# Fourier blocks of 80 instead of 48 in a two-layer graph kernel, with the stages set in another order

## The chip, the cores and the metric

The kernel runs on one core of a Trainium2 chip. The metric is device time in microseconds (us) of one execution. The core has five engines with a queue of instructions each: TensorE (PE, matrix products; its weight loads are PEld), VectorE (DVE), ScalarE (ACT), GpSimd (POOL) and SyncE (SP, which here only issues DMAs). Each works its queue off in order and waits on semaphores where an operand comes from another engine or from a DMA. Matmuls write to PSUM, which has eight banks of 128 partitions by 512 float32; DVE and ACT empty them into SBUF.

## The reference, cut to what matters

The input is `x` of 128 graphs with 128 nodes and 256 channels, float32. Two layers are computed, each as x + layer(relu(layernorm(x))).

```
# layer 0, on h = relu(layernorm(x)) and its channels-first form hc
c = relu(bn1(conv1d(hc, conv1_w)))            # kernel size 1
x_conv = relu(bn2(conv1d(c, conv2_w, pad 8)) + hc)    # 17 taps along the nodes, 256 to 256 channels
s = h @ w_se.T + b_se;  A = exp(-|s_i - s_j|^2) * adj
x_nmp = A @ relu(h @ w_msg.T + b_msg)         # the neighbour part
gi = [x_conv, x_nmp] @ w_ih.T + b_ih;  gh = h @ w_hh.T + b_hh
r, z = sigmoid(gi_r + gh_r), sigmoid(gi_z + gh_z)
x = x + (1 - z) * tanh(gi_n + r * gh_n) + z * h
# layer 1, on the first 25 nodes of each graph: five groups of nodes, each two normalized graph
# convolutions (256 to 512 to 256) with relu, fused with softmax weights and added to x
```

The convolution with 17 taps is the largest piece. Both kernels compute it by a short Fourier transform along the nodes. The 128 nodes of a graph are cut into blocks of F - 16 outputs, each block is transformed with F points (a matmul with a constant matrix), each frequency is multiplied by the spectrum of the taps (a 256 by 256 complex product), and the result is transformed back.

## The kernel before, in words

With F = 48 a block gives OB = 32 outputs, so a graph has NB = 4 blocks, and 128 columns of a product hold BG = 32 graphs: NBAT = 4 batches of BQ = 8 groups. A group `q` is GB = 4 graphs; there are NQ = 32. There are NF + 1 = 24 frequency steps: the first holds the two real ones, and each of the other 23 a complex one as three real products.

The pieces of work are Python generators:

- `stage_a(q)` (L366) loads a group, normalizes it (`moments` L270, `normalize` L281), transposes it on PE (`ph`, L383), writes hT to DRAM (`hTd`, L390), does the first convolution (`pc`, L396; its eviction `h`, L399 and L401) and the forward transform (`pf`, L409; evicted by DVE at L415 and ACT at L417 into `X`).
- `tap_weights()` (L438) makes the tap spectra: 128 matmuls `pw` (L454) with 17 rows each on four groups of 32 rows, evicted by ACT (L457) and DVE (L458) into `ws`, which goes to DRAM as `wfd` (L463).
- `stage_b(bat)` (L476) does the products of one batch: it loads `wf` from `wfd`, forms sums on POOL (L496, L497), multiplies (`pa`, `pb`, L502), and writes `y` to DRAM as `yd`.
- `neighbours(q)` (L566) computes x_nmp (`pse` L572, `pm` L592, `pd` L604 and L606, `px` L617). `early(q)` (L623) does it ahead for the first batch and leaves the result in DRAM (`xmd`).
- `stage_n(q)` (L638) gets hT and x_nmp for the gates: from DRAM for the first batch, by computing the neighbour part for the others. `stage_c(q)` (L659) transforms back (`pi`, L678), computes the gates (products `p`, L713, and `pg`, L777), with Sigmoid and Tanh on ACT and the last sums on POOL, and writes out.
- `prepare(blk)` and `block(blk)` are layer 1, in eight blocks of 16 graphs (`py`, `ph`, `pz`, `pg`, `pfu`, from L1001 on). A block needs the four groups of gates that it covers.

The order in which all these stand in the engines' queues is fixed when the program is made. `Order.run` takes several lanes of generators. A generator yields two numbers: PE time that it has just put into the queue, and time until its next part can run. The lane that has received least PE time for its weight is next, if its next part is ready on this planned clock. `ahead` is the number of generators of a lane under way at once. Nothing is reordered on the chip.

Before, the first eight `stage_a` run beside `tap_weights`, then the products of batch 0 beside the eight `early`. After that the gates start, and transforms and products of batches 1 to 3 are a lane beside the gates (weight 0.5); layer 1 is a lane beside the gates once the last batch has its products:

```
    groups = Lane([stage(q) for q in range(NQ) for stage in (stage_n, stage_c)], ahead=2)
    side = Lane(first, weight=0.5)
    order.run(groups, side, beside, until=side)
    order.run(groups, Lane(second, ahead=2, weight=0.4))
```

Of the kernel before, what the change touches and what calls it, by code (L numbers as in the profile page):

```python
# [23 lines left out]
F = 48  # L24
# [6 lines left out]
HB = NB // 2 * F  # L31
# [28 lines left out]
def _fourier():  # L60
# [7 lines left out]
    inv = np.zeros((P, OB * NB // 2))  # L68
# [10 lines left out]
    for b in range(NB // 2):  # L79
        s = slice(b * OB, (b + 1) * OB)  # L80
        inv[b * F, s], inv[b * F + 1, s] = 1 / F, (-1.0) ** i / F
        for f in range(1, NF + 1):
            th = 2 * np.pi * ((f * i) % F) / F
            inv[b * F + 2 * f, s] = 2 / F * np.cos(th)
            inv[b * F + 2 * f + 1, s] = -2 / F * np.sin(th)
# [5 lines left out]
    tap4 = np.zeros((P, 64))  # L91
    for r in range(4):
        tap4[32 * r:32 * r + TAPS, :F] = tap
# [86 lines left out]
class Order:  # L180
# [6 lines left out]
    def run(self, *lanes, until=None):  # L187
        for lane in lanes:
            lane.done = 0.0
        while True:  # L190
# [13 lines left out]
            lane.done += step[0]  # L204
            r[1] = self.now + step[1]
# [3 lines left out]
def kernel(ctx: ExitStack, tc: tile.TileContext, x, adj, consts, vecs, w_se, conv1_w,  # L209
# [15 lines left out]
    xmd = [dr.tile([P, 2, 512], FP, name=f"xmd{q}") for q in range(BQ)]  # L225
# [25 lines left out]
    c1w = wp.tile([P, 2, D], FP, name="c1w")  # L251
# [12 lines left out]
    brow = cp.tile([P, D], FP, name="brow")  # L264
# [4 lines left out]
    def moments(src, tag):  # L269

        st = f2.tile([P, 4, 6], FP, tag=tag + "st", name="st")
        mv = f2.tile([P, 4, 2], FP, tag=tag + "mv", name="mv")
        rs = f2.tile([P, 4], FP, tag=tag + "rs", name="rs")
        for t in range(4):
            nc.vector.bn_stats(st[:, t], src[:, t])
            nc.vector.bn_aggr(mv[:, t], st[:, t])
        nc.vector.tensor_scalar(rs, mv[:, :, 1], EPS, None, op0=ALU.add)  # L277
        nc.gpsimd.tensor_tensor(rs, rs, c("mhalf")[:, :4], ALU.pow)  # L278
        return mv, rs
# [68 lines left out]
    lab = ExitStack()  # L348
    ab = lab.enter_context(tc.tile_pool(name="ab", bufs=2, side="right"))
    xf = lab.enter_context(tc.tile_pool(name="xf", bufs=1, side="right"))  # L350
    LATE = {}
    X = xf.tile([P, 2, F, P], FP, name="X")
    XA, MOM, LOADED = {}, {}, set()
    A_DONE, B_DONE, G_DONE, C_DONE = set(), set(), {-1}, set()

# [5 lines left out]
    def load_xa(q):  # L361
        LOADED.add(q)
        XA[q] = ab.tile([P, 4, D], FP, tag="xa", name=f"xa{q}")
        load_x(XA[q], q)

    def stage_a(q):  # L366

        while q // BQ and q // BQ - 1 not in B_DONE:
            yield 0.0, 1.0
        for n in range(q, min(q + 2, NQ)):  # L370
            if n not in LOADED:
                load_xa(n)
        if q not in MOM:
            MOM[q] = moments(XA[q], "a")
            normalize(XA[q], XA[q], *MOM[q])
            yield 0.0, 6.0
        xn = XA.pop(q)
        nxt = q + 1 if q + 1 < NQ else None
        hT = ab.tile([P, 2, 512], FP, tag="hTa", name=f"hTa{q}", bufs=1)
# [8 lines left out]
        if q + 2 < NQ:  # L388
            load_xa(q + 2)
        nc.gpsimd.dma_start(out=hTd[q], in_=hT)  # L390
        h1 = ab.tile([P, GB, D], FP, tag="h1", name=f"h1{q}", bufs=1)
        for h in range(2):
# [9 lines left out]
            if h and nxt:  # L402
                MOM[nxt] = moments(XA[nxt], "a")
            yield 1.75, 1.6 * h
        for h in range(2):
# [12 lines left out]
            if h and nxt:  # L418
                normalize(XA[nxt], XA[nxt], *MOM[nxt])
            yield 1.3, 1.5 * h  # L420
# [3 lines left out]
    mid = ExitStack()  # L424
# [4 lines left out]
    def load_taps(n, *engines):  # L429

        wt = tw.tile([P, 16, D], FP, tag="wt", name=f"wt{n}", bufs=4)
# [6 lines left out]
    def tap_weights():  # L438


        yield 0.0, 0.0
        for n in range(4):
            if n == 1:
                load_taps(3, nc.sync, nc.gpsimd)
                load_late()
            for m in range(8):
                if m % 4 == 0:
                    ws = tw.tile([P, 2, 8, D], FP, tag="ws", name=f"ws{n}_{m}")
                pws = [ptmp.tile([P, 2, D], FP, tag="tmp", name=f"pw{n}_{m}_{h}")
                       for h in range(2)]  # L450
                for r in range(4):
                    rows = slice(32 * r, 32 * r + TAPS)
                    o = r % 2 * 64
                    nc.tensor.matmul(pws[r // 2][o:o + 64], c("tap")[rows],  # L454
                                     wts[n][rows, 2 * m:2 * m + 2], start=True, stop=True)
                i = m % 4 * 2
                nc.scalar.activation(ws[:, 0, i:i + 2], pws[0], AF.Copy)  # L457
                nc.vector.tensor_copy(ws[:, 1, i:i + 2], pws[1])  # L458
                yield 0.9, 1.2
                if m % 4 == 3:  # L460
                    for r in range(4):
                        o, i0 = r % 2 * 64, 64 * r + 16 * n + 2 * (m - 3)
                        nc.gpsimd.dma_start(out=wfd[:, i0:i0 + 8], in_=ws[o:o + F, r // 2])  # L463
# [6 lines left out]
        LATE["io"] = ctx.enter_context(tc.tile_pool(name="io", bufs=2, reuse_waits="tile"))  # L470
        LATE["fr"] = ctx.enter_context(tc.tile_pool(name="fr", bufs=1, reuse_waits="tile"))
        LATE["xf"] = lab.enter_context(
            tc.tile_pool(name="xw", bufs=3, side="right", reuse_waits="tile"))


    def stage_b(bat):  # L476
        while not all(q in A_DONE for q in range(bat * BQ, (bat + 1) * BQ)):
            yield 0.0, 0.5
        while "xf" not in LATE:
            yield 0.0, 0.5  # L480
        if bat == 0:
            yield 0.0, 12.0
        WF, xf = {}, LATE["xf"]

        def load_w(f):
            w = WF[f] = xf.tile([P, 2, 3, D], FP, tag="wf", name=f"wf{bat}_{f}")
# [17 lines left out]
        for f in range(2):  # L504
            load_w(f)
        yield 0.0, 4.0
        late = None
        for f in range(NF + 1):
            if f + 2 <= NF:
                load_w(f + 2)  # L510
# [3 lines left out]
            pa = ptmp.tile([P, 2, D], FP, tag="tmp", name=f"pa{bat}_{f}")  # L514
# [21 lines left out]
    IN, IN2, X1, E_DONE = {}, {}, {}, set()  # L536
# [10 lines left out]
    def sums(name, q, x, bufs=1):  # L547


        t = LATE["fr"].tile([P, 4, D], FP, tag=name, name=f"{name}{q}", bufs=bufs)  # L550
# [6 lines left out]
    def load_yt(q, h):  # L557

        if q < NQ and q // BQ in B_DONE:
            IN2[q, h] = LATE["io"].tile([HB, GB, D], FP, tag="yt", name=f"yt{q}_{h}")  # L560
            x0 = (q % BQ * 2 + h) * GB
            nc.sync.dma_start(
                out=IN2[q, h],
                in_=yd[q // BQ].rearrange("(x b) f c -> (b f) x c", b=NB // 2)[:, x0:x0 + GB])
# [58 lines left out]
    def early(q):  # L623
# [3 lines left out]
        if q not in IN:  # L627
            IN[q] = load_n(q)
            yield 0.0, 6.0
        hT, ad = IN.pop(q)  # L630
        if q + 1 < BQ and q + 1 in A_DONE:
            IN[q + 1] = load_n(q + 1)
# [5 lines left out]
    def stage_n(q):  # L638
        if q < BQ:
            while len(E_DONE) < BQ:  # L640
                yield 0.0, 0.5
            hT = LATE["io"].tile([P, 2, 512], FP, tag="hT", name=f"hT{q}")
            nc.sync.dma_start(out=hT, in_=hTd[q])
            xm = LATE["fr"].tile([P, 2, 512], FP, tag="xnmp", name=f"xms{q}", bufs=2)
            nc.sync.dma_start(out=xm, in_=xmd[q])
            yield 0.0, 4.0
            HT[q] = hT
        else:
            while q not in A_DONE:
                yield 0.0, 1.0  # L650
            hT, ad = load_n(q)
            yield 0.0, 4.0
            HT[q] = hT
# [495 lines left out]
```

## Time and profile before

| | us |
|---|---|
| median of three runs | 2195.71 (2195.38 to 2197.89) |
| span of the profiled execution | 2200.9 |
| PE busy | 2117.9 |
| DVE, POOL, ACT busy | 1166.1, 791.8, 730.5 |
| products (L502 `pa`, `pb`), busy | 181.9, 94.5 |
| forward transforms (L409), busy | 99.7 |
| tap spectra on PE (L454), busy | 40.7 |
| DMA | 259.65 MB, mean 118 GB/s |

A row of the page gives line, engine, operation, names of the result and the operands, shapes, count, busy time and mean duration of one. A float32 matmul leaves two records on PE. Matmuls overlap in the pipeline, so the mean duration of a record is longer than the time that it holds PE; the latter is the distance from start to start in the timeline.

### The profile page before, as it was taken

The page shows a single profiled execution, that of the slowest core. Times are in us where ns is not written, and L with a number is a line of the kernel's source. Part 1 is how long each engine was busy: PE and PEld are TensorE (multiplying, and loading weights), DVE is VectorE, ACT ScalarE, POOL GpSimd, SP SyncE. Part 2 cuts the span into 40 slices and gives each one's busy share as a digit, 9 for nine tenths or more (in the row PEclk, how much of TensorE's full clock was granted, in tenths as well). Part 3 has the DMA queues.
Part 4 walks back from the last instruction along what each step waited for, and adds up shares of the span by engine and source line. Part 5 has one row for each costly group of instructions (what it writes and reads, how often), then busy time and mean ns, then how long its engine had stood idle before and what let it go on. Part 6 is the DMA issues. An engine that isn't in the chain of part 4 may idle for free.

```text
span 2200.9 us, 30725 instructions
## 1 busy us (share of the span) xinstructions
PE 2117.9 (96%) x11308; PEld 1678.9 (76%) x11308; DVE 1166.1 (53%) x2659; ACT 730.5 (33%) x1519; POOL 791.8 (36%) x978
## 2 busy tenths in 40 slices
PE   6979999999999999999999999899999999999997
PEld 3558868888888888888788888677786777877765
DVE  4544446645556555445665455655464555554442
ACT  2432233322234432334342323323334233233332
POOL 2217613355522245542224555413223323213330
PEclk9989999999999999999999999999999999999999
DMA  9868643455532344533224446222222223212221
GB/s 173 239 197 288 236 105 91 149 164 162 162 101 87 106 139 144 153 120 106 76 79 149 128 154 167 60 80 60 77 77 78 67 68 87 70 52 63 87 68 49
DMA packets 193977, 259.65 MB, mean 118 GB/s; under 512 B 21981, under 2 KB 157154, under 8 KB 192290
## 3 DMA queue, kind: packets, MB, share of 16 engines
q1 hardware_dynamic: 165682, 175.89, 28.2%
q0 software_dynamic: 27312, 81.03, 12.2%
q8 instruction: 90, 1.47, 0.3%
q10 hardware_dynamic: 832, 0.75, 0.2%
q14 instruction: 61, 0.50, 0.1%
HBM read 178.44 MB, written 79.17 MB: 117 GB/s over the span
## 4 chain that ended last, share of the span: by engine, by line
PE 86%; DVE 6%; DMA 3%; ACT 1%; POOL 1%; issue 1%; SPq 0%; DVEq 0%; ACTq 0%; POOLq 0%
PE p L713 34%; PE pa L502 8%; PE pg L777 5%; PE pm L592 4%; PE ph L1018 4%; PE pc L396 4%; PE pz L1027 4%; PE pb L502 4%; PE pf L409 3%; PE pi L678 2%; PE px L617 2%; PE pg L1060 1%; PE pc L692 1%; PE po L829 1%; PE py L1001 1%; PE ph L383 1%
## 5 line engine op out<-in xcount | busy, mean ns | idle before, releaser
L502 PE MATMUL pa<-wf,X 128*128 128x256 f32 x768 | 181.9, 380 | 0.0
L278 POOL TENSOR_TENSOR rs<-rs,cst 128x4 f32<-128x4 f32 x40 | 41.3, 1032 | 334.3 <-DVE rs L277 327.2
L502 PEld LDWEIGHTS pa<-wf,X 128*128 128x128 f32 x768 | 144.6, 190 | 22.1 <-issue 2.4
L813 POOL TENSOR_TENSOR d<-hT,r 128x512 f32<-128x512 f32 x64 | 82.2, 1285 | 215.0 <-ACT r L810 215.0
L525 DVE SCALAR_TENSOR_TENSOR y<-pa,kk 128x512 f32<-128x512 f32 x92 | 63.5, 690 | 156.0 <-ACT kk L524 155.9
L713 PE MATMUL p<-tc,wrz 128*128 128x256 f32 x512 | 132.0, 380 | 5.0 <-DVE tc L552 5.0
L713 PE MATMUL p<-th,wrz 128*128 128x256 f32 x512 | 134.1, 385 | 0.0
L713 PE MATMUL p<-tm,wrz 128*128 128x256 f32 x512 | 132.3, 381 | 0.0
L592 PE MATMUL pm<-wmsg,hT 128*128 128x256 f32 x512 | 123.7, 386 | 0.0
L497 POOL TENSOR_TENSOR wf<-wf 128x512 f32<-128x512 f32 x92 | 116.6, 1268 | 18.9 <-DMA wf<-wfd 18.9
L496 POOL TENSOR_TENSOR xs<-X 128x256 f32<-128x256 f32 x92 | 67.8, 737 | 154.6 <-PE pb L502 130.9
L396 PE MATMUL pc<-c1w,hTa 128*128 128x256 f32 x512 | 122.1, 385 | 0.2 <-DVE h L399 0.2
L777 PE MATMUL pg<-hT,whn 128*128 128x512 f32 x256 | 121.2, 599 | 0.0
L396 PEld LDWEIGHTS pc<-c1w,hTa 128*128 128x128 f32 x512 | 96.9, 192 | 22.6 <-ACT ws L457 5.7
L1018 PE MATMUL ph<-yz,w 128*128 128x96 f32 (+3 forms) x640 | 110.7, 326 | 3.4 <-DVE aT L609 1.6
L592 PEld LDWEIGHTS pm<-wmsg,hT 128*128 128x128 f32 x512 | 97.7, 194 | 20.9 <-issue 8.2
L713 PEld LDWEIGHTS p<-tc,wrz 128*128 128x128 f32 x512 | 97.5, 191 | 19.0 <-DVE tc L552 5.8
L524 ACT ACTIVATE kk<-pb 128x256 f32<-128x256 f32 x92 | 35.3, 383 | 225.5 <-PE pb L502 225.5
L1018 PEld LDWEIGHTS ph<-yz,w 128*128 128x128 f32 x640 | 88.1, 193 | 26.5 <-issue 15.7
L713 PEld LDWEIGHTS p<-tm,wrz 128*128 128x128 f32 x512 | 98.0, 191 | 13.4
L1027 PE MATMUL pz<-hh,w 128*128 128x96 f32 (+3 forms) x640 | 107.4, 322 | 0.0
L713 PEld LDWEIGHTS p<-th,wrz 128*128 128x128 f32 x512 | 94.8, 191 | 15.9 <-issue 3.5
(205 smaller groups left out, 4614.2 us busy)
## 6 DMA issues: line engine op xcount, KB each, us to landing
wf<-wfd SPq DMA_DIRECT2D x192, 256.0 KB, 3.2
yd<-y POOLq DMA_DIRECT2D x96, 256.0 KB, 2.5
yt<-yd SPq DMA_DIRECT2D x64, 384.0 KB, 4.4
hT<-hTd SPq DMA_DIRECT2D x40, 512.0 KB, 5.6
w<-in_W SPq DMA_DIRECT2D x40, 512.0 KB, 3.7
xa<-in_x SPq DMA_DIRECT2D x128, 128.0 KB, 4.6
hTd<-hTa POOLq DMA_DIRECT2D x32, 512.0 KB, 4.5
xt<-in_x SPq DMA_DIRECT2D x128, 128.0 KB, 2.8
```

The source lines that it names most:

```text
L396: nc.tensor.matmul(pc[:, i], hT[:, k, (2 * h + i) * N:(2 * h + i + 1) * N], c1w[:, k], start=(k == 0), stop=(k == 1))
L409: nc.tensor.matmul(pf[:, i, :F * NB], h1[:, 2 * h + i, k * P:(k + 1) * P], fwd, start=True, stop=True)
L496: nc.gpsimd.tensor_tensor(XS[f], X[:, :, 2 * f], X[:, :, 2 * f + 1], ALU.add)
L497: nc.gpsimd.tensor_tensor(WF[f][:, :, 2], WF[f][:, :, 0], WF[f][:, :, 1], ALU.add)
L502: nc.tensor.matmul(ps, xk(k), WF[f][:, k, s], start=(k == 0), stop=(k == 1))
L525: nc.vector.scalar_tensor_tensor(y, pa, 2.0, kk[:, None].to_broadcast([P, 2, D]), op0=ALU.mult, op1=ALU.subtract)
L592: nc.tensor.matmul(pm[:, i], hT[:, k, j * N:(j + 1) * N], wmsg[:, k], start=(k == 0), stop=(k == 1))
L713: nc.tensor.matmul(ps[:, m], w[:, i, k, m * P:(m + 1) * P], factor(i, x, t), start=first and j == 0, stop=last and j == len(n) - 1)
L777: nc.tensor.matmul(pg, whn[:, k, dc * P:(dc + 1) * P], hT[:, k], start=(k == 0), stop=(k == 1))
L813: nc.gpsimd.tensor_sub(d, hT[:, dc], r[:, dc])
L1018: nc.tensor.matmul(ph, w1[:, k, m * P:(m + 1) * P], yz[:, k, :, o:o + n], start=(k == 0), stop=(k == 1))
L1027: nc.tensor.matmul(pz, w2[:, g, m, cc * P:(cc + 1) * P], hs[g][:, m], start=(m == 0), stop=(m == 3))
```

## The change: longer blocks in two batches, and another order

With F = 80 a block gives 64 outputs, a graph has two blocks, and 128 columns of a product hold 64 graphs: two batches of 16 groups, 40 frequency steps each. The aim is fewer products for the same outputs, since more of each block is output and less is overlap. The spectra of the taps get 80 rows instead of 48. A pair of them no longer fits the 128 partitions of a PSUM bank, so each of the four matmuls of a step has a bank of its own (three from the pool of the gates' banks).

`X` for 16 groups takes the room that the gates had. So both batches are transformed and multiplied first, with all neighbour parts beside them (`early` for all 32 groups, results in `xmd`). `stage_n` then only loads. Gates come after that, with layer 1 as a lane beside them from near their start. The buffers of transforms (`ab`) and products (`xw`) take turns in one place; up to three `stage_a` are under way, with four buffers `xa`; weights of the lanes are new.

```diff
-F = 48
+F = 80
...
-xmd = [... for q in range(BQ)]
+xmd = [... for q in range(NQ)]
...
 def load_xa(q):
-        XA[q] = ab.tile([P, 4, D], FP, tag="xa", name=f"xa{q}")
+            XA[q] = LATE["ab"].tile([P, 4, D], FP, tag="xa", name=f"xa{q}", bufs=4)
...
 def tap_weights():
-                pws = [ptmp.tile([P, 2, D], FP, tag="tmp", name=f"pw{n}_{m}_{h}")
-                       for h in range(2)]
+                pws = [(pgat if r < 3 else ptmp).tile([P, 2, D], FP, tag="gat" if r < 3 else "tmp",
+                                                      name=f"pw{n}_{m}_{r}") for r in range(4)]
...
-                nc.scalar.activation(ws[:, 0, i:i + 2], pws[0], AF.Copy)
-                nc.vector.tensor_copy(ws[:, 1, i:i + 2], pws[1])
+                for r in range(4):
+                    if r < 2 or (r == 2 and m % 2):
+                        nc.scalar.activation(ws[:F, r, i:i + 2], pws[r][:F], AF.Copy)
+                    else:
+                        nc.vector.tensor_copy(ws[:F, r, i:i + 2], pws[r][:F])
...
 def stage_b(bat):
-            w = WF[f] = xf.tile([P, 2, 3, D], FP, tag="wf", name=f"wf{bat}_{f}")
+            w = WF[f] = xf.tile([P, 2, 3, D], FP, tag="wf", name=f"wf{bat}_{f}", bufs=4)
...
-        for f in range(2):
+        for f in range(3):
             load_w(f)
...
-            pa = ptmp.tile([P, 2, D], FP, tag="tmp", name=f"pa{bat}_{f}")
+            pa = pgat.tile([P, 2, D], FP, tag="gat", name=f"pa{bat}_{f}")
...
 def stage_c(q):
-                nc.tensor.matmul(pi[b * 64:(b + 1) * 64], inv[:HB], yt[:, b::2],
+                nc.tensor.matmul(pi[b * 64:(b + 1) * 64], inv[:F], yt[:, b::2],
...
-    begin = Lane([stage_a(q) for q in range(BQ)], weight=1.5)
-    beside = Lane([tap_weights()] + [early(q) for q in range(BQ)])
...
+    beside = Lane([tap_weights()] + [early(q) for q in range(NQ)])
+    gates = Lane([fold_gates()], weight=0.5)
+    for bat, (during_a, during_b) in enumerate(((0.66, 0.5), (0.2, 0.65))):
+        if bat:
+            take_turn("ab", 2, reuse_waits="tile")
+        begin = Lane([stage_a(q) for q in range(bat * BQ, (bat + 1) * BQ)], ahead=3)
+        beside.weight = during_a
+        order.run(begin, beside, *[gates] * bat, until=begin)
+        take_turn("xw", 3, reuse_waits="tile")
+        products = Lane([stage_b(bat)])
+        beside.weight = during_b
+        order.run(products, beside, *[gates] * bat, until=products)
...
-    side = Lane(first, weight=0.5)
-    order.run(groups, side, beside, until=side)
-    order.run(groups, Lane(second, ahead=2, weight=0.4))
+    beside.weight = 0.5
+    order.run(groups, beside, Lane(second, ahead=2, weight=0.36))
```

## The prediction

> **What bounds the kernel now.** I read the page from the top: busy shares, slices, the chain of waits, and then stretches of the span for where TensorE (PE) stands still.
>
> ```profile
> PE 2117.9 (96%) x11308; PEld 1678.9 (76%) x11308; DVE 1166.1 (53%) x2659; ACT 730.5 (33%) x1519; POOL 791.8 (36%) x978
> ...
> PE   6979999999999999999999999899999999999997
> ...
> PEclk9989999999999999999999999999999999999999
> DMA  9868643455532344533224446222222223212221
> ...
> PE 86%; DVE 6%; DMA 3%; ACT 1%; POOL 1%; issue 1%; SPq 0%; DVEq 0%; ACTq 0%; POOLq 0%
> ```
>
> PE is busy 96% of the span and holds 86% of the chain; no other engine passes 53%. So the time is PE's work plus PE's idle time, 2201 - 2118 = 83 us. The slices show the idle time in the first seventh and the last slice. A busy PE isn't PE at its peak, so work has to be priced from starts in the timeline, not from the mean durations.
>
> The table of stretches (us, then busy time of PE, PEld, DVE, ACT, POOL, granted clock, DMA share, GB/s) tells where the 83 us lie:
>
> ```profile
> 0.00:17.00 17.00, 1.05 (x5) 1.05 (x6) 4.54 (x24) 1.28 (x1) 4.03 (x9) 1.00 0.98 136
> 17.00:125.00 108.00, 97.48 (x544) 56.62 (x543) 60.26 (x154) 44.49 (x81) 30.57 (x51) 0.94 0.91 220
> 125.00:170.00 45.00, 34.07 (x228) 27.78 (x227) 20.09 (x52) 12.30 (x31) 4.70 (x7) 0.85 0.65 207
> 170.00:275.00 105.00, 104.38 (x618) 89.76 (x616) 49.15 (x89) 26.77 (x69) 72.81 (x86) 1.00 0.76 255
> ```
> ```profile
> 440.00:1320.00 880.00, 871.76 (x4422) 720.35 (x4420) 479.79 (x1045) 289.74 (x594) 374.08 (x452) 1.00 0.43 127
> 1320.00:1540.00 220.00, 211.41 (x1140) 165.95 (x1138) 126.96 (x286) 72.73 (x152) 80.11 (x101) 0.98 0.34 92
> 1540.00:2060.00 520.00, 513.62 (x2818) 394.69 (x2818) 275.97 (x640) 181.40 (x378) 152.05 (x185) 0.99 0.25 70
> 2060.00:2191.00 131.00, 123.94 (x772) 90.86 (x771) 48.18 (x129) 42.62 (x97) 26.42 (x39) 0.99 0.24 72
> 2191.00:2201.00 10.00, 0.00 (x0) 0.00 (x0) 0.00 (x0) 0.00 (x0) 2.17 (x4) 0.61 0.21 53
> ```
>
> Idle PE: 16 us at the start, 10.5 in the stretch of transforms and tap spectra (17 to 125), 11 around the first neighbour parts (125 to 170), 0.6 in the first products, 5 in 275 to 330 (same view, not shown), 8 in 440 to 1320, where transforms and products lie beside gates, 8.6 when layer 1 starts, 6.4 in gates beside layer 1, 7 in three blocks of layer 1 that are left over at the end, 10 after the last matmul. Where different work lies side by side PE loses 1%; where transforms stand with little beside them it loses 10%.
>
> **What the Trainium skill says.** (1) "TensorE: Matmul & The Clock Gate", Part 1 (the HAM clock gate), says that PE runs at half clock after an idle window of some 3.4 us. The trace agrees: after the 4.04 us gap at 38.1 us four records of pw take 1.97 us where elsewhere eight take 1.09, and the granted clock is 0.85 in 125 to 170. (2) The same page, Part 3 (packing small matmuls), says that matmuls on different groups of 32 rows run at once, four of 512 columns 3.07 times faster. Agrees: four tap matmuls (8 records) take 1.02 us from start to start, while 8 records of 512 columns one after the other take 3.4 us (8 x 0.43, from the starts of pg L777). (3) "TensorEngine Tiling (Array Packing)", Gotcha 1 (PSUM pressure), says that different row tiles must write to different banks. The change obeys this with four banks. No page prices a mix of DMA like that of the first 150 us; there I use the trace alone.
>
> **The change, part by part.**
>
> Prices come from the timeline of PE:
>
> ```profile
> 186.25 1.03 PE L502 MATMUL pb<-wf,xs 128*128 128x256 f32 x4
> 187.11 1.05 PE L617 MATMUL px<-aT,msg 128*128 128x128 f32 x8
> ...
> 1103.15 1.47 PE L409 MATMUL pf<-cst,h 128*128 128x192 f32 x8
> 1104.45 1.03 PE L713 MATMUL p<-th,wrz 128*128 128x256 f32 x4
> ```
>
> Four records of 256 columns hold PE 187.11 - 186.25 = 0.86 us, 0.216 each; a matmul is two records. Eight of 192 columns hold it 1.30 us, 0.163 each.
>
> *Products (L502).* Before, four batches of 4 + 23 x 6 = 142 matmuls: 1136 records, as the page has them (768 + 368). After, two batches of 4 + 39 x 6 = 238: 952. Removed 184 x 0.216 = **-39.7 us**, all on PE in the stretch where it is 99% busy, so all on the path.
>
> *Forward transforms (L409).* The same 512 records, 80 x 2 = 160 columns instead of 192: 0.163 x 160/192 = 0.136, so 512 x 0.027 = **-13.8 us**.
>
> *Inverse (L678).* 80 rows instead of 96, the same 512 columns and the same two column halves: 0.
>
> *Tap spectra (L454).* 128 matmuls as before, now 80 output columns each into a bank of its own. Unseen before with so many output columns on four row groups at once; the nearest row is pd<-lr (32*128), whose four start 7 ns apart. So they still run together: 0. If they went two by two it would be 64 sets x 0.43 = +27 us. I take 0.
>
> *Evictions of the tap spectra.* 128 instead of 64, of 512 columns: ACT 80 x 0.60 = 48 us (19 before), DVE 48 x 0.69 = 33 (22). Their wait on PE is hidden as long as ACT and DVE keep up, below.
>
> *Order.* All 32 transforms now stand in two stretches of 16 and no longer beside gates. In the order of the changed program's PE instructions the taps end when 14 transforms have begun; then 4 neighbour parts come before the first products, 9 stand among them, 6 among the second 16 transforms, 10 among the second products, and 3 are left. Seven of the eight blocks of layer 1 stand among the gates and one is alone at the end (three before).
>
> A transform holds PE 8 x 0.109 + 16 x 0.216 + 16 x 0.136 = 6.5 us and DVE 4 x (0.40 + 0.18 + 0.44) + 0.19 + 2 x 0.69 + 0.46 = 6.1 us (means of its rows, an upper bound). Beside gates this DVE load was spread; alone it is 94% of PE's. Three transforms under way instead of one and four xa buffers are what can hide the latencies.
>
> DMA until the taps end: wfd 80 x 256 KB = 21.0 MB (12.6 before), hTd 14 x 0.52 = 7.3, x 8.4, taps 4.5, constants and the like 1.3: 42.5 MB. PE needs 13.5 x 6.5 + 39 (pw's share of PE before) = 127 us after its 16 us of start: 143. The trace shows 220 GB/s at a share of 0.91 in 17 to 125, with the same kinds of small packets, and 288 in 165 to 220 (page: slice 4). At 220 the bytes take 193 us, at 288 148. I take 270: 157 us, 14 us more than PE, and 6 for stalls. What queues behind it: PE's pw waits for banks that ACT and DVE empty into ws, ws waits for its wfd write, and ACT's next hTa stands behind it in its queue.
>
> Idle PE after, by estimate: start 16; taps 20; to the first products 6; products 1 + 1; to the second transforms and back 4 + 3; second transforms 16 x 6.5 + 6 x 7.1 (a neighbour part: pse 0.6, pm 3.5, pd 1.2, px 1.8) = 147 at 8%: 12; gates beside layer 1: 8.6 for its start and 1.2% of 1200 (as 6.4 of 520): 23; the last block 7/3 = 2; end 10. Sum 98, **+15 us** against 83.
>
> Hidden: 24 more xmd writes and hT and xm reads (0.5 MB each; DMA share 0.25 among gates); sum products on POOL (80 instead of 96 sets of 2.0 us, under 3.9 us of PE each); fewer switches between Exp and Sigmoid tables (x24 and x25 of 1.28 us on an ACT busy 33%).
>
> Sum: -39.7 - 13.8 + 15 = -38.5; 2195.7 - 38.5 = **2157**.
>
> **The rivals.** *Smooth*: the deeper transforms hide everything. Then taps 10.5 idle as before, transitions 9, second transforms 5, gates 15, products 2, start 16, tail 12: 70, and 2195.7 - 53.5 - 13 = **2129**. For it: 1% idle wherever work was mixed. Against: PE, DVE and DMA all want over 90% of the tap stretch. *Starved*: DMA stays at 220 GB/s, so taps end at 193 us, and idle there is 193 - 143 = 50 instead of 20; and the second transforms wait on DVE as at 267 to 278 us, where one alone took 10.9 us for 7 of work; a quarter of that loss, 16, comes on top. 2157 + 30 + 16 = **2203**, slower than before. For it: the clock of 0.94 and DMA share of 0.91 in 17 to 125 with 8.4 MB fewer to write. Against: the rate there was held down by the tap loads to few partitions, which don't grow.
>
> **How the numbers follow.** Forecast 0.56, smooth 0.26, starved 0.18. Range 2122 to 2203: under it some of smooth, over it the worse half of starved (with taps two by two in it). Faster by over 0.2% (under 2191): forecast, smooth and a sliver of starved, 0.82; within 0.03; slower 0.15.
>
> **What would show it.** Products x640 + x312 records; pf near 0.136 us from start to start; pw's four still within 10 ns; PE busy near 2064 us. Idle PE of some 36 us before the first products and under 12% in the second transforms; waits of ACT and DVE for wfd small; one block alone at the end. Wrong if the tap stretch ends well after 165 us, if PE's clock falls under 0.95 in the second transforms, or if gates beside layer 1 idle more than 2%.

## The result, and the profile after

The changed kernel takes 2214.86 us (median of four runs, 2211.64 to 2222.41) against 2195.55 for the kernel before on the same chip: ratio 1.0091 [1.0062, 1.0119]. It is slower by 0.9%. The forecast was 2157 with a range up to 2203, so both the side and the range were wrong. A repetition on another chip, e6 below, gives 1.0077 [1.0064, 1.0091].

The page of the changed kernel, with the lines that answer to those of before (busy times, slices, chain of waits):

```profile
PE 2079.8 (94%) x11124; PEld 1636.9 (74%) x11124; DVE 1198.4 (54%) x2659; ACT 690.1 (31%) x1511; POOL 788.4 (36%) x990
...
PE   4999999899999999999999999999999999999967
...
PEclk8999999999999999999999999999999999999988
DMA  9986777744777734323232333232332322332211
...
PE 83%; DVE 7%; DMA 4%; issue 2%; POOL 2%; ACT 1%; SPq 1%; DVEq 0%; ACTq 0%; POOLq 0%
```

PE's work fell, 2117.9 to 2079.8 us, and the span rose, 2200.9 to 2210.7. So idle PE rose from 83 to 131 us. The chain says the same: DVE, DMA, issue and POOL together went from 11% to 15%. The slices hardly show where, because a wait of 5 us in a slice of 55 us leaves the digit at 9. One has to cut the span into stretches (us, then busy time of PE, PEld, DVE, ACT, POOL, granted clock, DMA share, GB/s):

```profile
0.00:19.00 19.00, 3.45 (x16) 3.36 (x16) 6.30 (x29) 1.76 (x2) 4.13 (x9) 1.00 1.02 144
19.00:45.00 26.00, 10.88 (x40) 6.24 (x39) 10.30 (x31) 4.15 (x9) 6.80 (x7) 0.63 0.83 130
45.00:180.00 135.00, 127.36 (x732) 85.34 (x730) 90.26 (x237) 76.84 (x159) 51.76 (x85) 0.96 0.84 250
...
414.00:575.00 161.00, 154.98 (x1000) 137.05 (x1001) 110.15 (x290) 69.97 (x155) 40.62 (x47) 0.98 0.48 159
...
940.00:2140.00 1200.00, 1165.93 (x5734) 893.21 (x5734) 652.96 (x1389) 350.59 (x739) 397.33 (x487) 0.98 0.30 82
2140.00:2156.00 16.00, 3.09 (x10) 2.38 (x11) 4.99 (x16) 0.00 (x0) 10.57 (x10) 0.50 0.11 25
2156.00:2197.00 41.00, 38.32 (x239) 28.88 (x237) 9.05 (x22) 14.04 (x32) 0.00 (x0) 0.96 0.11 39
2197.00:2211.00 14.00, 0.00 (x0) 0.00 (x0) 0.11 (x1) 0.00 (x0) 2.26 (x4) 0.61 0.15 37
```

Set against the forecast's list of idle PE (length of a stretch less PE's busy time; four stretches of the same view are not shown):

| stretch | forecast | measured |
|---|---|---|
| start and taps (0 to 180) | 16 + 20 = 36 | 15.5 + 15.1 + 7.6 = 38.2 |
| to the first products (180 to 237) | 6 | 6.2 |
| products | 2 | 0 |
| turn and second transforms (396 to 575) | 4 + 12 = 16 | 8.8 + 6.0 = 14.8 |
| back to the gates, gates beside layer 1 (745 to 2140) | 3 + 23 = 26 | 8.2 + 34.1 = 42.3 |
| last block and end (2140 to 2211) | 2 + 10 = 12 | 12.9 + 2.7 + 14 = 29.6 |
| sum | 98 | 131 |

The stretches that I had argued about, the taps and the transforms, came out as forecast. The gates and the end, taken over from the kernel before at a rate, gave 34 us more.

**The gates.** Seven waits of 4.58 to 4.85 us stand in the gates, one for each block of layer 1 but the last, at 941, 1116, 1292, 1467, 1644, 1819 and 1995 us. The distance is four groups of gates, some 176 us, so every block meets the same part of a group (five times at the sum L777, as below, and twice a little later, at L783). The timeline at the first of them (start, duration, instruction, and in brackets the idle time before it and what ended it):

```profile
936.01 1.04 POOL L275 TENSOR_TENSOR rs<-rs,cst 128x4 f32<-128x4 f32 x1 [8.60 <-DVE rs L274]
937.08 1.38 DVE L280 TENSOR_SCALAR x1h<-x,mv,rs 128x256 f32<-128x256 f32 x4 [1.16 <-POOL rs L275]
...
940.56 0.41 DVE L777 TENSOR_TENSOR v<-v,p 128x256 f32<-128x256 f32 x1
941.00 0.42 DVE L778 TENSOR_TENSOR r<-r,v 128x256 f32<-128x256 f32 x1
...
941.02 1.22 PE L698 MATMUL p<-tm,wn 128*128 128x256 f32 x2 [4.84 <-DVE v L777]
```

PE needs the PSUM bank that DVE empties with `v` (L777), a sum of 0.41 us. In the last group, with nothing in the way, this sum comes 0.94 us after the ACT copy before it (L775, 2131.02 and 2131.96); here that copy was at 933.62, so with nothing ahead of it the sum could have started near 934.6, and it starts at 940.56. PE has stood still since 936.2. In DVE's queue ahead of it stand the four `moments` of the block's rows (933.5 to 935.9), then `normalize` (L280), which waits 1.16 us for a power on POOL (L275) and takes 1.38, then the sums `tm` of the next group (938.4 to 940.6), whose operand `xm` was only sent for at 929.73. Nothing here is long. It is mostly work of layer 1 placed as one piece in the queue of an engine that is only 54% busy, ahead of the one instruction that PE waits for; e12 below shows what the sums `tm` add.

**The end.** The last group of gates now has nothing beside it:

```profile
2140.85 0.48 PE L814 MATMUL po<-cst,z 128*128 128x128 f32 x1 [4.68 <-POOL z L801]
2144.75 1.76 PE L814 MATMUL po<-cst,z 128*128 128x128 f32 x7 [3.42 <-POOL z L801]
2155.14 5.01 PE L986 MATMUL py<-r,x1h 128*128 128x212 f32 x16 [8.64 <-POOL x1h L901]
```

The chain from the last gate through POOL's sums to the output's transposes, and then from x1 through DRAM, DVE and POOL to the last block's first product, stands bare: 16.7 us. Before, three blocks of layer 1 were left over here and covered it.

**The clock.** The priced work alone was to bring PE to 2064 us; it is 2079.8. After each of these waits the clock is at half for a while (two records from 941.02 to the next start at 942.04: 1.02 us, where two take 0.43). The "TensorE: Matmul & The Clock Gate" page of the Trainium skill, Part 1, says that an idle window of about 3.4 us has this effect. The trace agrees for these waits, which are over that, but here less is enough too (columns as above, the last three numbers are the clock, the DMA share and GB/s):

```profile
237.30:240.70 3.40, 3.40 (x9) 2.70 (x8) 1.03 (x5) 0.82 (x5) 0.00 (x0) 0.50 0.00 0
...
1322.00:1326.00 4.00, 4.00 (x27) 3.44 (x26) 1.94 (x3) 1.46 (x4) 0.00 (x0) 1.00 0.01 4
1326.10:1329.50 3.40, 3.40 (x10) 2.68 (x9) 0.75 (x5) 0.00 (x0) 2.08 (x3) 0.51 0.00 0
```

The first of these stretches follows a wait of only 1.64 us (at 235.7). The last follows no wait: PE was busy for 4 us before it, in part with 16 records of a small product of layer 1 (`pa<-cst,b`, L935).

The product `p` (L698) held PE 813.5 us in 3584 records, 796.3 before: 17 us that I had nowhere in the sum. Taken record by record, what `p` held above 0.216 us each is 19.5 us in records at half clock (8.2 before) and 19.8 us in records at full clock (13.9 before). So about 11 of the 17 are the clock; the cause of the other 6 is open.

**Start and turn.** Two smaller waits have a like form. At 38 us a bank of the tap spectra is not emptied (DVE `ws`, L462), since DVE stands in the statistics of a group that has not arrived:

```profile
35.18 0.43 DVE L272 BATCH_NORM_STATS2 st<-xa 128x6 f32<-128x256 f32 x1 [10.51 <-DMA xa<-in_x]
...
38.25 1.99 PE L455 MATMUL pw<-wt,cst 17*80 17x512 f32 x4 [15.12 <-DVE ws L462]
```

And at 414 us PE waits 8.33 us for `ph` of the second batch, with three groups' statistics in a row in DVE's queue ahead of the scaling.

### The profile page after: what moved, and what is told of

It is laid out like the page before. It is cut to its first block, busy times and chain, and to the rows that moved or that the text cites. A ratio compares the mean times of both kernels' runs of the same rounds, so it can differ in the third digit from the quotient of the medians.

```text
span 2210.7 us, 30635 instructions
## 1 busy us (share of the span) xinstructions
PE 2079.8 (94%) x11124; PEld 1636.9 (74%) x11124; DVE 1198.4 (54%) x2659; ACT 690.1 (31%) x1511; POOL 788.4 (36%) x990
## 4 chain that ended last, share of the span: by engine, by line
PE 83%; DVE 7%; DMA 4%; issue 2%; POOL 2%; ACT 1%; SPq 1%; DVEq 0%; ACTq 0%; POOLq 0%
PE p L698 33%; PE pa L502 6%; PE pg L762 5%; PE ph L1003 5%; PE pz L1012 5%; PE pm L591 4%; PE pc L401 4%; PE pb L502 3%; PE pi L663 3%; PE px L616 2%; PE pf L412 2%; DMA xa<-in_x 2%; PE pg L1045 1%; PE pc L677 1%; DVE st L272 1%
## 5 line engine op out<-in xcount | busy, mean ns | idle before, releaser
L798 POOL TENSOR_TENSOR d<-hTc,r 128x512 f32<-128x512 f32 x64 | 84.3, 1317 | 508.4 <-ACT r L795 495.7
L502 PE MATMUL pa<-wf,X 128*128 128x256 f32 x640 | 154.2, 385 | 0.0
L698 PE MATMUL p<-tc,wrz 128*128 128x256 f32 x512 | 133.0, 382 | 1.5 <-DVE tc L552 1.0
L698 PE MATMUL p<-th,wrz 128*128 128x256 f32 x512 | 134.2, 385 | 0.0
L698 PE MATMUL p<-tm,wrz 128*128 128x256 f32 x512 | 133.2, 383 | 0.0
L502 PEld LDWEIGHTS pa<-wf,X 128*128 128x128 f32 x640 | 119.3, 192 | 17.5 <-issue 2.8
L275 POOL TENSOR_TENSOR rs<-rs,cst 128x4 f32<-128x4 f32 x40 | 42.0, 1049 | 250.7 <-DVE rs L274 243.6
L525 DVE SCALAR_TENSOR_TENSOR y<-pa,kk 128x512 f32<-128x512 f32 x78 | 53.8, 690 | 142.7 <-ACT kk L524 142.5
L401 PE MATMUL pc<-c1w,hTa 128*128 128x256 f32 x512 | 127.6, 399 | 0.3 <-ACT hTa L392 0.3
L401 PEld LDWEIGHTS pc<-c1w,hTa 128*128 128x128 f32 x512 | 98.3, 199 | 29.2 <-issue 6.4
L711 ACT ACTIVATE r<-r,brz 128x256 f32<-128x256 f32 x128 | 58.0, 500 | 186.5 <-DVE r L742 157.3
L762 PE MATMUL pg<-hTc,whn 128*128 128x512 f32 x256 | 116.0, 593 | 0.0
L826 POOL DMA_DIRECT2D x1d<-xt x112 | 59.3, 530 | 150.5 <-DVE xt L820 147.2
L698 PEld LDWEIGHTS p<-tc,wrz 128*128 128x128 f32 x512 | 97.5, 192 | 17.9 <-DVE tc L552 4.7
L698 PEld LDWEIGHTS p<-tm,wrz 128*128 128x128 f32 x512 | 98.5, 192 | 13.7
L698 PEld LDWEIGHTS p<-th,wrz 128*128 128x128 f32 x512 | 94.8, 190 | 16.9 <-issue 4.9
L698 PE MATMUL p<-tm,wn 128*128 128x256 f32 x256 | 80.6, 397 | 24.2 <-DVE v L777 24.2
```

The lines of the kernel that those rows point to most:

```text
L401: nc.tensor.matmul(pc[:, i], hT[:, k, (2 * h + i) * N:(2 * h + i + 1) * N], c1w[:, k], start=(k == 0), stop=(k == 1))
L502: nc.tensor.matmul(ps, xk(k), WF[f][:, k, s], start=(k == 0), stop=(k == 1))
L525: nc.vector.scalar_tensor_tensor(y, pa, 2.0, kk[:, None].to_broadcast([P, 2, D]), op0=ALU.mult, op1=ALU.subtract)
L698: nc.tensor.matmul(ps[:, m], w[:, i, k, m * P:(m + 1) * P], factor(i, x, t), start=first and j == 0, stop=last and j == len(n) - 1)
L711: nc.scalar.activation(dst[:, m], src[:, m], AF.Sigmoid, bias=brz[:, b + m:b + m + 1])
L762: nc.tensor.matmul(pg, whn[:, k, dc * P:(dc + 1) * P], hT[:, k], start=(k == 0), stop=(k == 1))
```

## The experiments

The theories. **Order**: the work saved is saved, and the time is lost in a few short waits that the new order makes by where it puts layer 1 and the statistics in DVE's queue; each can be moved. **DMA**: the new first 180 us are bound by transfers, as the rival "starved" has it. **Depth or length**: the blocks of 80 themselves, or three transforms under way, cost something. All edits are against the changed kernel, except e4; e9 and e10 are shown as edits of e5. All ratios are to the kernel before on the same chip. Most expectations missed in size, and some in direction; where one did, it is said below.

| kernel | median us | ratio [95%] |
|---|---|---|
| e6, the changed kernel again | 2212.93 | 1.0077 [1.0064, 1.0091] |
| e1, layer 1 held back three groups | 2196.2 | 0.9993 [0.9980, 1.0006] |
| e2, rows of layer 1 in pieces | 2192.2 | 0.9979 [0.9966, 0.9991] |
| e8, both | 2182.42 | 0.9941 [0.9927, 0.9954] |
| e7, transforms started one after the other | 2204.95 | 1.0043 [1.0031, 1.0056] |
| e5, all three | 2169.12 | 0.9879 [0.9866, 0.9893] |
| e10, all three, held back two groups | 2178.78 | 0.9910 [0.9892, 0.9927] |
| e9, e5 with half of the spectra's bytes | 2159.81 | 0.9818 [0.9798, 0.9839] |
| e12, rows of layer 1 later | 2198.41 | 1.0002 [0.9987, 1.0016] |
| e11, later, held back two groups, transforms one after the other | 2149.98 | 0.9781 [0.9759, 0.9802] |
| e3, two transforms under way | 2280.26 | 1.0374 [1.0352, 1.0396] |
| e4, the new order on blocks of 48 | 2309.69 | 1.0506 [1.0478, 1.0534] |

**e6, the changed kernel again**, for the size of what is to be explained:

> The changed kernel once more, beside the others on one chip. Both theories: ratio to the kernel before 1.006 to 1.012; a sum of waits as in its first trace. It sets the level from which the edits are counted.

It repeats: 2211.6 us of span, the same seven waits of 4.58 to 4.85 us, the same end (4.68, 3.42, 8.64), 14.59 at the start.

**e1, holding layer 1 back by three groups** so that blocks are left to cover the end:

```diff
+LAG = 3
-        ready = all(q in C_DONE for q in range(blk * QS, (blk + 1) * QS))
+        last = min((blk + 1) * QS + LAG, NQ)
+        ready = all(q in C_DONE for q in range(blk * QS, last))
```

> The changed kernel, but a block of layer 1 waits for three more groups of gates than it reads, so that about two blocks instead of one are left at the end. Theory A (the end is long because the last group's gates have nothing beside them: PE waits 4.7 + 3.4 + 8.6 us there): these three waits shrink under 3 us in all, the span falls by 10 to 16 us to some 2200, and the seven waits of 4.8 us among the gates stay, because the rows of layer 1 still come at the same place of a group. Rival B (all layer 1 that is left at the end runs as badly as the last block does): no gain, within 4 us.

The three waits of the end are gone; the last wait over 1 us is one of 2.66 at 2096. In the gates six waits of 4.58 to 4.84 remain, one block now lying in the end. The gain against the changed kernel is 0.84 to 0.98% (from e6's ratio or the first one), 18 to 21 us. That is the 16.7 us of bare waits, and a little more; 10 to 16 were expected.

**e2, the rows of layer 1 in pieces**, so that DVE gets no run of four statistics and four scalings at once:

```diff
-        normalize(x1h, X1[blk], *moments(X1[blk], "b"))
...
+        for t in range(4):
+            nc.vector.bn_stats(st[:, t], X1[blk][:, t])
+            nc.vector.bn_aggr(mv[:, t], st[:, t])
+            yield 0.0, 2.0
...
+        yield 0.0, 3.0
+        for t in range(4):
+            nc.vector.tensor_scalar(x1h[:, t], X1[blk][:, t], mv[:, t, 0:1], rs[:, t:t + 1],
+                                    op0=ALU.subtract, op1=ALU.mult)
+            yield 0.0, 2.0
```

> The changed kernel, but the layer-1 normalization of a block (moments, power on GpSimd, scaling) is cut into nine pieces which the planner spreads over DVE's queue instead of one run of it. Theory A (PE waits 4.8 us in each of seven blocks because this run, 5 us with its wait for GpSimd, and the sums of the next group stand in DVE's queue before the operand that frees PE's bank): the seven waits fall under 1.5 us each, PE's half-clock windows after them go too, and the span falls by 30 to 45 us, to 2170 to 2185. Rival B (DVE is simply short of time in that part of the gates): the waits come back in other places, PE idle between 940 and 2140 us stays above 25 us, and the gain is under 12 us.

The 4.8 us waits are gone, and the end is still bare (1.34, 3.57, 8.66). The gain is 0.98 to 1.12%, some 21 to 25 us, under the 30 to 45 expected; PE's busy time is 2074.0, 6 less for the same instructions. But the pieces made new waits, smaller: in five blocks a pair of about 1.03 and 2.15 us at `p<-xc,wrz`. The timeline at one of them:

```profile
1285.79 1.26 POOL L798 TENSOR_TENSOR d<-hTc,r 128x512 f32<-128x512 f32 x1 [17.71 <-ACT r L795]
1285.99 1.34 DVE L551 TENSOR_TENSOR th<-hTc 128x256 f32<-128x256 f32 x1
...
1292.62 1.65 DVE L680 SCALAR_TENSOR_TENSOR xc<-pc,s_bn,hTc 128x256 f32<-128x256 f32 x4
...
1293.69 2.64 PE L698 MATMUL p<-xc,wrz 128*128 128x256 f32 x11 [1.03 <-ACT xc L683]
```

The pieces now delay DVE's sums by a little, until those run beside POOL's; there they take 1.3 to 1.5 us in place of 0.42, and the `xc` behind them come late.

**e8, both edits:**

> The changed kernel with two edits, layer 1 three groups behind and its normalization in nine pieces. Theory A (two separate waits): gains add up, 40 to 50 us under the changed kernel, ratio to the kernel before 0.987 to 0.992. Rival B (the late layer 1 and the spread rows take away the same wait): no more than 28 us under the changed kernel, ratio 0.996 or above.

It gains 0.0136 on e6 in the same comparison, 30 us. The two gains alone add up to 39 to 46, so they overlap, and the result lies between the two theories. The trace shows how: only one pair of waits is left in the gates (1.03 and 2.13), but two at the end, 5.00 and 3.48 at `po`, came back. The pieces take so long on the planned clock that block 6 comes after the last `po`.

**e7, the transforms started one after the other**, against the waits at 38 and 414 us:

```diff
+        if q % BQ in (1, 2) and q > 1:
+            yield 0.0, 12.0 if q == 2 else 4.0 * (q % BQ)
```

> The changed kernel, only with the second and third transforms of each batch started later on the plan. Theory A (15 us near 23 us and 8 us near 406 us are moments that stand too early in DVE's queue): first wait under 6 us, second under 4 us, the rest of the transforms as before, span shorter by 10 to 18 us. Rival B (DMA brings nothing earlier in the first 40 us): the wait at the start stays over 10 us with another releaser; gain 4 to 6 us from the second place alone.

The gain on e6 is 0.0034, 7 us, less than the 10 to 18 expected and less than the waits taken away. The wait of 15 us at 38 is gone, but 3.10 at 61.6, 6.76 at 82.8 and 2.21 at 104.9 stand in its place: the stretch 17 to 180 has 17 us idle, against 23. The wait of 8.33 at 414 became 1.16 and 2.35. So more than a half of the first wait moved on, as it would if something besides DVE's order bounds that stretch; e9 tests that.

**e5, all three edits:**

> The changed kernel with three edits: layer 1 three groups of gates behind, its normalization in nine pieces, and the second and third transforms of each batch started later on the plan (8 and 12 us), so that their moments come after the first evictions. Theory A (the miss is waits from the order in the queues, each with its own place): the gains of the two measured edits add up, 21 + 25 us, and the third brings 10 to 18 us: 2135 to 2165, ratio to the kernel before 0.973 to 0.986, half-clock time under 45 us. Rival B (PE's idle time only moves): about as the better of the single edits, 2185 to 2195.

0.9879, just short of what theory A expected, and 13 us better than e8: stagger, worth 7 alone, is worth more here.

**e9, the same with half of the spectra's rows written to and read from DRAM** (the lower 40 of 80 rows, read twice): the bytes of the first stretch go down by 10.5 MB, with PE's work unchanged.

```diff
-                        nc.gpsimd.dma_start(out=wfd[:, i0:i0 + 4], in_=ws[:F, r])
+                        nc.gpsimd.dma_start(out=wfd[:F // 2, i0:i0 + 4], in_=ws[:F // 2, r])
...
-                nc.sync.dma_start(out=w[:, k, :2], in_=wfd[f::NF + 1, k * P:(k + 1) * P]
-                                  .rearrange("s p o -> p s o"))
+                for s in range(2):
+                    nc.sync.dma_start(out=w[:, k, s], in_=wfd[f, k * P:(k + 1) * P])
```

> The kernel with all three edits (layer 1 three groups behind, normalization in pieces, transforms staggered), which here writes only the first 40 of the 80 rows of the tap spectra to DRAM and reads those twice in the products: it leaves out half of the spectra, so its output is not the convolution. Theory A (up to 180 us DMA is the bound: staggering the transforms took away the 15 us wait and brought waits of 2 to 7 us at 42 to 108 us instead): 10.5 MB less, PE idle between 17 and 180 us falls from some 18 to under 9 us, the first products start 8 to 15 us earlier, and the span falls by as much against the kernel with all three edits (2169). Rival B (those waits are moments, evictions and banks in the order of the queues): idle time there stays within 4 us, gain under 4 us.

The stretch 17 to 180 us of e5 and then of e9 (columns as above):

```profile
17.00:180.00 163.00, 144.47 (x772) 95.64 (x771) 100.46 (x269) 82.84 (x169) 59.53 (x91) 0.92 0.86 234
```
```profile
17.00:180.00 163.00, 151.05 (x820) 101.85 (x820) 105.75 (x284) 86.45 (x176) 63.39 (x97) 0.95 0.76 190
```

PE gets 6.6 us more work done in it, the last `pw` comes at 170.2 us in place of 178, the wait of 5.66 us at 86 shrinks to 1.43 at 79, the first products start at 224.9 us in place of 235.7, and the ratio is 0.0061 lower, 13 us. Idle PE in the stretch is 12 us where theory A wanted under 9. A quarter of the bytes less is worth 13 us of some 160, so DMA is a part of the bound there, but not the whole of it. This part of "starved" holds, at less than half of the 30 us that it put there.

**e10, e5 with two groups in place of three**, meant to keep the pieces and take away the end's two waits:

```diff
-LAG = 3
+LAG = 2
```

> All three edits, with layer 1 two groups behind instead of three, so that block 6 stands before the last group's transposes in PE's order and not after them. Theory A (at the end PE waits 5.0 and 3.5 us for GpSimd's last sums because block 6 came after them): these two waits shrink to under 2 us in all, span 6 to 9 us shorter, 2160 to 2163. Rival B (then block 7 stands alone and its own waits return): within 3 us of 2169.

The end's two waits are gone, and still the kernel is slower than e5, 0.9910 against 0.9879 (the intervals just touch), which neither theory expected. With two groups the pieces meet the sums again: 1.03 and 2.12 us in nearly every block, where e5 has one pair. One constant in the order changes where all of layer 1 lands.

**e12, the rows of layer 1 not in pieces, but later**: the planned time of their load is 20 us, no longer 6.

```diff
             load_x1(blk)
-            yield 0.0, 6.0
+            yield 0.0, 20.0
```

> The changed kernel with one edit: the planner waits 20 instead of 6 us after a block's load, so that the normalization of layer 1 stays one run of DVE work but stands behind the transposed convolution of the next group, where PE has other gates to go on with. Theory A (only the place matters): the waits of 4.8 us are gone or under 1.5 us, gain as with nine pieces, 18 to 28 us under the changed kernel, 2186 to 2196. Rival B (one run of 5 us is too long wherever it stands): waits of 3 to 5 us come back at another line in most blocks, gain under 8 us.

Six of the seven blocks now leave a wait of 0.93 to 1.03 us at `p<-tc,wrz`, behind the rows' new place. Four longer waits remain: 2.96 us at 1660 (`ph<-yz`), and 2.01, 2.18 and 3.58 us at the old place, `p<-tm,wn` (936, 1797 and 1974 us). No work of layer 1 stands ahead of `v` there any more. The next group's sums `tm` do, and they wait for a load:

```profile
1972.52 0.42 DVE L551 TENSOR_TENSOR tm<-xm 128x256 f32<-128x256 f32 x1 [4.24 <-DMA xm<-xmd]
...
1973.99 0.41 DVE L777 TENSOR_TENSOR v<-v,p 128x256 f32<-128x256 f32 x1
```

That load was issued at 1964.93, 7.6 us before the first sum; in most groups the distance is 16 us or more. So the rows were the larger part of the seven waits, but in some blocks not all of it: what stands ahead can also be an instruction whose own operand is late. The gain is 0.0075 on e6, 16 us, without one engine instruction more or less, where 18 to 28 were expected. So the seven waits are in the main a matter of place and not of the work.

**e11, later, with two groups and the stagger:**

> Layer 1 two groups behind, transforms staggered, and the normalization in one run at the other place instead of in pieces. Theory A: as fast as the kernel with pieces and two groups behind, within 6 us of it, 2158 to 2168, ratio to the kernel before 0.982 to 0.988. Rival B (one run costs more than pieces): 8 us or more slower than it.

It is the fastest of all: 0.9781 [0.9759, 0.9802], 48 us under the kernel before. It differs from e10 only in that the rows come later and not in pieces, and that is worth 0.0129, 28 us, where theory A expected at most 6 either way. Its busy times, and its gates beside layer 1 among the stretches:

```profile
PE 2069.3 (96%) x11124; PEld 1630.0 (76%) x11124; DVE 1191.9 (56%) x2659; ACT 682.2 (32%) x1509; POOL 790.3 (37%) x990
```
```profile
940.00:2050.00 1110.00, 1100.30 (x5400) 843.67 (x5399) 625.58 (x1337) 326.40 (x700) 383.71 (x472) 0.99 0.31 85
```

9.7 us idle in 1110, 0.9%, against 34 in 1200; idle PE in the whole span is 2144.6 - 2069.3 = 75 us. Six of the blocks now leave 1.0 us, on `tc` (one of the others leaves 2.99 us at 1703, `ph<-yz`), and none waits for `xm`; the timeline at one of the six:

```profile
1169.00 1.03 PE L701 MATMUL p<-tm,wrz 128*128 128x256 f32 x4
1171.07 1.13 PE L701 MATMUL p<-tc,wrz 128*128 128x256 f32 x4 [1.04 <-DVE tc L555]
```

**e3, two transforms under way in place of three:**

```diff
-        begin = Lane([stage_a(q) for q in range(bat * BQ, (bat + 1) * BQ)], ahead=3)
+        begin = Lane([stage_a(q) for q in range(bat * BQ, (bat + 1) * BQ)], ahead=2)
```

> The changed kernel with two transforms under way instead of three. Theory A (the 15 us wait near 23 us and the 8 us wait near 406 us come from moments of the third group, which stand in DVE's queue ahead of evictions and of the first group's scaling): the first wait falls under 5 us, the second under 4 us, the span falls by 12 to 20 us, if the transforms lose less than 5 us elsewhere. Rival B (DMA is short in the first 40 us whatever the order): the first wait stays above 10 us under another name, gain under 6 us, and the transforms after it get more idle time.

62 to 65 us slower than the changed kernel, by the ratios, where theory A expected 12 to 20 us faster. From 119 to 213 us every second transform waits 4 to 6 us (5.75, 4.67, 4.91, 4.88 at `ph`), the second ones leave 21 of 208 us idle at a clock of 0.91. Since the lanes move on a clock of their own, the neighbour parts are then used up too early (argued from the code): at 838 us PE waits 13.69 us for `yt`, the first inverse transform, with nothing to put in. So the depth of three carries the transforms, as the forecast had assumed, though part of this loss is that of the turn.

**e4, the kernel before with the new order but blocks of 48** (four batches, one transform under way as in before, `stage_n` only loading):

```diff
-    beside = Lane([tap_weights()] + [early(q) for q in range(BQ)])
...
+    beside = Lane([tap_weights()] + [early(q) for q in range(NQ)])
+    for bat, (during_a, during_b) in enumerate(((0.66, 0.5), (0.2, 0.65), (0.2, 0.65), (0.2, 0.65))):
+        begin = Lane([stage_a(q) for q in range(bat * BQ, (bat + 1) * BQ)])
...
+    order.run(groups, beside, Lane(second, ahead=2, weight=0.36))
```

> The kernel before with blocks of 48, but in the order of the changed kernel: all transforms, products and neighbour parts first, then gates with layer 1 beside them from near their start. Theory A (the order costs, the longer blocks gain): slower than before by 30 to 60 us, 2225 to 2255, with waits of 4 to 5 us among the gates in most blocks and a bare end of some 15 us. Rival B (the longer blocks themselves cost, by more spectra to write and evict): within 10 us of before.

112 us slower than before, about twice the most that theory A expected. It has the same seven waits (4.84 to 5.81) and the same end (4.68, 3.57, 8.65), with blocks of 48: they belong to the order and not to the length. The rest of its loss is its own: transforms one deep, where two were too few in e3; PE's work, busy 2162.4 us for the 11308 records that took 2117.9 before, at a mean clock of 0.970 in place of 0.983; and 16.85 us at 868, where the products end and no neighbour part is left to bridge to the gates. So it does not measure the order of the changed kernel by itself. Blocks of 80 in the old order were not tried, since `X` of 16 groups does not fit beside the gates.

## Why the prediction was wrong

*Priced work: right.* The page has x640 + x312 records of the products. From start to start they held PE 210.5 us, 246.6 before: 36 less, where 39.7 was forecast. `pf` stands 0.136 us apart and held 78.0 against 91.3: 13.3 less, where 13.8 was forecast. Tap spectra, four of 80 columns still 7 ns apart, held 38.1 against 39.1: nothing, as taken. (The separate banks that the prediction's third citation asks for were not what let them run together: before, two of the four row groups wrote to the two halves of one bank, L453, and those four started 7 ns apart as well.) The inverse, taken as 0, gave 3.

*PE busy near 2064: wrong, 2079.8.* The sum took all work outside the change to hold PE as long as before. For `p` that is 17 us too few, 11 of them by the half clock. e11, whose only two waits over 3.4 us come before 63 us, brings `p` back to 794.6. The kernel before had such stretches too: from 1097.5 to 1100.9 us its granted clock is 0.50, behind a wait of 2.15 us. So its trace held the term that I left out. The first convolution `pc` (L401) went from 114.1 to 121.4 us and stays at 122.5 in e11. It lies in the transforms of the tap stretch: the 216 records of `pc` before 180 us stand 0.252 us apart in the mean, against a median of 0.216, where the clock is 0.63 and then 0.96. Before, only 112 of its 512 records lay in such a stretch (0.241).

*Idle before the first products, second transforms: right,* as the table shows, with the clock at 0.98 in the latter. The tap stretch ended at 179.6 and not by 165, which the prediction named as a sign against it. Its idle time is as forecast all the same; it is PE's work in it that is longer, 141.7 us where 127 was priced, for the same 14 transforms. That fits the same fault, a price at full clock in a stretch where the clock is 0.63 and 0.96.

*Gates beside layer 1: the step that failed first.* I took "8.6 for its start and 1.2% of 1200", 1.2% being measured in a stretch in which layer 1 had a backlog. The one wait at this place came at its start, the same `p<-tm,wn` on the same DVE sum, and I priced it as a start, once:

```profile
1405.17 1.22 PE L713 MATMUL p<-tm,wn 128*128 128x256 f32 x2 [3.54 <-DVE v L792]
```

The second block's rows cost 2.82 us at another place (`p<-tc,wrz`, 1451 us); the next four stood at four further places in DVE's queue, with no wait over 0.9 us near them. In the new order each block is released by the group just finished, so it comes to the same part of a group seven times. The idle time is 34 us in place of 23, 2.8% of the stretch, past the 2% that the prediction had named as a sign against it. With the 17 us of `p` some 28 are missing. That a backlog is what spread before's later blocks over other places is argued from the code; that place decides is shown by e12 and e11.

*The end: the second step that failed.* "The last block 7/3 = 2" took the blocks left over for a cost. They were cover. With one block left the waits of the last group and of the last block are bare: 29.6 in place of 12. e1 shows it.

*The sum.* Forecast -38.5; the spans differ by +9.8. Of the miss of 48, 15 are PE's work, longer than its price (`p`, `pc`), 16 idle between 745 and 2140, 18 at the end, and -1 everywhere else. With the waits moved, e11 takes 2150 us. That this is near the forecast does not confirm it: e11 has edits, the stagger among them, that the forecast did not reckon with. What the starts of the records show is that the work saved on PE, 36 and 13 us, was there; the order gave it back.

*The rivals.* "Starved" named 2203, the nearest number, for other reasons: taps until 193 us and a loss in the second transforms, and neither came. Only its share in the first stretch is real (e9). "Smooth" took 15 us for the gates, and e11 gets 10 in 1110.

*Open.* Against e6, the stagger alone gains 7 us, holding back three groups 18, the later place 16, which is 41; e11, with two groups held back, gains 0.0296, 65. The edits move each other's work in the queues, and holding back two groups by itself was not run, so the 24 us between the two can't be divided among them. Some 8 of them may be e12's waits for `xm` (2.01, 2.18, 3.58), which e11 doesn't have. Nor were the later rows and the stagger tried on the kernel before, so the 48 us by which e11 beats it are not the worth of the longer blocks alone.

## What to carry to other kernels

When an order is changed, don't carry a rate of idle time over from the old one: ask for each short instruction that the bound engine waits for what will stand ahead of it in its engine's queue, whether that has its own operands by then, and how often the pattern repeats; a wait seen once at the start of a phase may be what each round of the new order pays. Work that is "left over" at the end may be the cover of a chain that has no other, so price the end with the chain bare. And look in the trace of before for stretches at half clock, and add for the slow work behind waits: here 17 us in one product, 11 of them by the clock, beside seven waits of 33 us in all.

## What the hardware showed that was not expected

- A kernel that is 94% busy still falls to the half clock, and not only behind its waits of 4.8 us: a wait of 1.64 us was followed by it, and so was a run of small matmuls with no wait at all (1326 us). In `p` it cost about 11 us more than before. In e2, where the waits are 1.0 and 2.2 us, PE's busy time is 5.8 us less for the same instructions.
- DVE's sums of two operands, 0.42 us alone, take 1.3 to 1.5 beside POOL's sums (1285.99 in e2: DVE ends at 1287.33, POOL at 1287.05). The "SBUF — State Buffer" page of the Trainium skill, section "SBUF: two separate sides", says that the two engines share a port pair as an exclusive lock for two-input operations; the trace agrees in that DVE's sum ends 0.28 us after POOL's. It doesn't agree everywhere: in the changed kernel a sum of 0.41 us (939.89) lies inside a POOL instruction recorded from 938.56 for 2.87 us. So 0.42 us is no safe price for such a sum while POOL is at sums of its own.
